# Cross-attention and gated feed-forward on one core: attention by 8 heads at a time, and a reordered query stage

## The chip, the cores and the metric

The kernel runs on one core of a Trainium2 chip. Its engines are TensorE (PE, with PEld for its weight loads), VectorE (DVE), ScalarE (ACT), GpSimd (POOL) and SyncE (SP, which issues most DMAs). Each engine takes its instructions in order and waits on semaphores for the others. The metric is the device time of one execution in microseconds (us), the median of several runs.

## What is computed

x is 16 x 128 x 1024 (16 blocks of 128 tokens), the context has the same shape; all is float32. Attention has 32 query heads of 32 channels in 8 groups, so that four query heads share one key and value head. Cut to what matters:

```python
def attn(q, k, v, w_q, w_k, w_v, w_out, mask):
    query, key, value = q @ w_q.T, k @ w_k.T, v @ w_v.T      # 32 heads; 8 groups; 8 groups
    scores = einsum('bghnd,bgsd->bghns', query, key) / 32**0.5
    scores = where(mask, scores, finfo.min)
    out = einsum('bghns,bgsd->bghnd', softmax(scores), value)
    return out @ w_out.T

x = x + attn(layernorm(x), ctx, ctx, w_q, w_k, w_v, w_out, mask)
x1, x2 = split(layernorm(x) @ w12.T + b12)
x = x + (silu(x1) * x2) @ w3.T + b3
```

## The kernel before

All large matrix products are done by fast schemes that trade a matrix product for sums of operands: seven products of half-sized parts in place of eight ("seven", numbers 1 to 7), in the query product and the first feed-forward product on two levels. A left sum (of weights or numbers) is named S or A_S, QS, QI; a right sum (of the streamed matrix) is named Y, Y_T, ctx_T or wo_T. These sums are made by DVE (through `nc.vector`) and POOL (through `nc.gpsimd`).

**The stages in time.** The first context products (keys and values of the first 8 blocks, `seven_round` with T = 0) end at about 58 us. The query stage follows, to about 246 us: 14 steps (`Q_STEPS`: outer number i in the order 1, 2, 3, 6, 5, 7, 4, for g = 0 and 1), each with seven inner products in the order 1, 5, 6, 7, 2, 3, 4, about 12 us of PE. Then attention, to about 612 us: for each of 16 token blocks t and each half gh of the heads, scores, softmax, turning and values; between these pieces PE works off a stream of other products, the second half of the context (`seven_round` with T = 1) and the output projection (`O_round`). The rest is the output projection's end and the feed-forward part.

**The query stage.** What goes with a step is written as a plan: `q_at(n, j, fn)` calls fn after product j of step n, and `q_follow` does it; n = -1 is the last context round. Within this stage the order on PE, DVE, ACT, POOL and SP is that of the program text. `q_outer_left(g)` makes the outer left sums 5, 6, 3, 7 of the query weights on POOL and stores them, with the parts for 2 and 4, to DRAM by six to eight DMAs on SP's queue (L517, L520); `q_load_left` (L193 through `load`) brings back the sum of a step two steps ahead; `q_inner_left` makes four inner left sums on POOL (L303, QI). `load_xq` loads the parts of x in turned form (xq). `q_outer_right` makes outer right sums on DVE (L488; its result overwrites an xq part or is a Y), `q_inner_right` the inner ones on DVE (L496, Y_T). In `seven`, L285 copies a bank, L288 and L290 make u1 and u3 from banks, and `done` in `q_step` adds to the kept sums (L579, L581, L586, L588). `centre(i)` takes the weights' mean off the query weights: sums on ACT, one matmul (L453), eight DVE instructions (L456). `feed_ctx` gives, in steps 11 to 13, one piece after another of the second context's loads and right sums (L243, two on DVE and two on POOL by pairs), with the loads and left sums of `wkv` put in between.

**Attention.** `scores(t, gh)` takes 16 heads: four banks, one for each of the key heads gl = 0 to 3; the loop runs over j (four query heads) outside and gl inside, so consecutive matmuls (L710) lie on rows 0, 32, 64, 96 onward of the array:

```python
for j in range(HPG):
    for gl in range(GL):
        rows = ds(gl * DH, DH)
        nc.tensor.matmul(
            ps[gl][:, j, :], QT[T, gh * HPG + j][rows, c, toks], KT[T, c][rows, gh, toks],
```

Then, for two banks at a time, DVE scales and masks (L719) and takes the maximum (L722), ACT makes the exponentials and their sums (L728), DVE the reciprocal (L734) and POOL scales the numbers (L737). `flip` turns the numbers of one gl (four transposes on PE, L743) and copies them out of the bank, on ACT (L746) or DVE (L748), to a temporary. `values` multiplies with V (L758, eight listed matmuls on four column groups), and ACT copies the result (L762). In the main loop an iteration takes the scores of one (t, gh), the values of two before, and the four flips of the one before; `stream.run(cost)` in between lets PE work off about so many us of the stream. A listed pair of matmuls of one kind is one float32 matmul of the program.

Buffers: 44 units of 1024 numbers for each partition, 14 temporaries of 512, 8 PSUM banks, each handed out in turn and waited for when all are taken.

Of the kernel before, what the change touches and what calls it, by code (L numbers as in the profile page):

```python
# [11 lines left out]
F32 = mybir.dt.float32  # L12
# [116 lines left out]
def xattn_ffn_kernel(  # L129
# [312 lines left out]
    def centre(i):  # L442


        ws, rows = raw_q[i], rows_in.pop(i)
        total = small.tile([P, 4], F32, tag="wm_sum", name=f"wm_sum_{i}", bufs=2)
        spread = temp([HC, P], f"wm_{i}")
        for r in range(4):
            nc.scalar.activation(rows[r], rows[r], AF.Identity, accum_out=total[:, r : r + 1])
            nc.scalar.activation(spread[:, r], ident, AF.Identity, scale=total[:, r : r + 1])  # L450
        yield 0.0
        ps = bank(f"wm_{i}").rearrange("p (r f) -> p r f", r=HC)
        nc.tensor.matmul(ps, mean_of, spread, start=True, stop=True)  # L453
        for q in range(4):
            for c in range(2):
                nc.vector.scalar_tensor_tensor(ws[q][:, :, c], ws[q][:, :, c], QSCALE, ps, ALU.mult, ALU.subtract)  # L456
        yield 0.87


# [17 lines left out]
    def q_outer_right(i, h, c):  # L477
        B11, B12, B21, B22 = (xq.get((2 * K + h, 2 * C + c)) for K in range(2) for C in range(2))
        y = Y.setdefault(i, {})
        if i in (1, 2, 3):  # L480
            y[h, c] = {1: B11, 2: B21, 3: B22}[i]
            return
        out, x, z = {
            5: (B11, B12, B11), 6: (None, B22, Y.get(5, {}).get((h, c))), 7: (B12, B22, B12),
            4: (B21, B21, Y.get(6, {}).get((h, c))),
        }[i]
        y[h, c] = out if out is not None else unit([2, 512], f"Y6_{h}_{c}")
        nc.vector.tensor_sub(y[h, c], x, z)  # L488

# [7 lines left out]

    q_left, q_inner, q_dram = {}, {}, {}

# [4 lines left out]
    def q_outer_left(g):  # L504
# [3 lines left out]
        for k, a, op, b in (  # L508
            (5, A21, "+", A22), (6, S[5], "-", A11), (3, A12, "-", S[6]), (7, A11, "-", A21),
        ):  # L510
            for h in range(2):
                x, z = (t[:, h] if t in (S[5], S[6]) else t[h] for t in (a, b))
                put(nc.gpsimd, S[k][:, h], x, op, z)
        for k in (2, 3, 6, 5, 7, 4):
            t = q_dram[g, k] = tc.dram_tile([P, 2, 2, 2, P], F32, name=f"QS{k}_dram_{g}")
            if k in S:
                nc.sync.dma_start(t, S[k])  # L517
            else:
                for h in range(2):
                    nc.sync.dma_start(t[:, h], {2: A12, 4: A22}[k][h])  # L520

# [4 lines left out]
    def q_inner_left(g, i, k):  # L526
        if i == 1:
            q_left[g, i] = q_part(g, 0, 0)
        A11, A12, A21, A22 = (q_left[g, i][h][:, r] for r in range(2) for h in range(2))
# [73 lines left out]
    def q_plans():  # L603
        for n, (g, i) in enumerate(Q_STEPS):
            if i != 1:
                q_at(n - 2, 3, q_load_left, g, i)
# [4 lines left out]
            if i == 1:  # L611
                q_at(0 if g else -1, 7, q_outer_left, g)
                q_at(n + 1, 2, q_store, g, i, "U")
# [36 lines left out]
        for m in (0, 1, 4, 5):  # L650
            q_at(12, 1 + m, q_home, 0, m)
        for j in range(1, 8):
            q_at(11, j, feed_ctx)
            q_at(12, j, feed_ctx)
            q_at(13, j, feed_ctx)

    def feed_ctx():
        if "ctx_1" not in feeds:
            feeds["ctx_1"] = Feed(ctx_work[1], 0)
        feeds["ctx_1"].give(1)  # L660

# [14 lines left out]
    def seven_round(T, k, R):  # L676
# [10 lines left out]
        def hook(j):  # L687
            tick()
            if (T, k, j) == (1, 0, 4):
                sums_left7(1, 1)  # L690
            if T == 1 and j in (1, 3):
                load_xs(NT + 2 * k + j // 2)
            if T == 1 and j in (4, 6):
                q_stats(NT + 2 * k + j // 2 - 2)
            transition(T, k, j)

        order = (1, 5, 6, 2, 7, 3, 4) if T else (1, 2, 5, 6, 7, 3, 4)
        yield from seven(left7.pop((T, k)), R, f"Q7_{T}_{k}", done, hook, order)

    OT, spilled = {}, {}  # L700

    def scores(t, gh):

        T, (c, i) = t // NT, divmod(t % NT, 4)
        toks, rstd = ts(i, S), mr[T][:, 1, t % NT : t % NT + 1]
        ps = [bank(f"s_{t}_{gh}_{gl}").rearrange("p (h k) -> p h k", h=HPG) for gl in range(GL)]
        for j in range(HPG):
            for gl in range(GL):
                rows = ds(gl * DH, DH)
                nc.tensor.matmul(  # L710
                    ps[gl][:, j, :], QT[T, gh * HPG + j][rows, c, toks], KT[T, c][rows, gh, toks],
                    start=True, stop=True,
                )
        numbers = []
        for two in range(2):
            nmax = small.tile([P, 2, HPG], F32, tag="nmax", name=f"nmax_{t}_{gh}_{two}")
            for e in range(2):
                s = ps[2 * two + e]
                nc.vector.scalar_tensor_tensor(  # L719
                    s, s, rstd, drop.unsqueeze(1).to_broadcast([P, HPG, S]), ALU.mult, ALU.add,  # L720
                )
                nc.vector.tensor_reduce(nmax[:, e], s, AX.X, ALU.max, negate=True)  # L722
            total = small.tile([P, 2, HPG], F32, tag="sum", name=f"sum_{t}_{gh}_{two}")
            for e in range(2):
                gl = 2 * two + e
                p = temp([HPG, S], f"p_{t}_{gh}_{gl}")
                for j in range(HPG):
                    nc.scalar.activation(  # L728
                        p[:, j, :], ps[gl][:, j, :], AF.Exp, bias=nmax[:, e, j : j + 1],
                        accum_out=total[:, e, j : j + 1],  # L730
                    )
                numbers.append(p)
            inv = small.tile([P, 2, HPG], F32, tag="inv", name=f"inv_{t}_{gh}_{two}")
            nc.vector.reciprocal(inv, total)  # L734
            for e in range(2):
                p = numbers[2 * two + e]
                nc.gpsimd.tensor_mul(p, p, inv[:, e].unsqueeze(2).to_broadcast([P, HPG, S]))  # L737
        return numbers

    def flip(bt, gh, gl, p):  # L740
        pt = bank(f"pt_{bt}_{gh}_{gl}").rearrange("p (h k) -> p h k", h=HPG)
        for j in range(HPG):
            nc.tensor.transpose(pt[:, j, :], p[:, j, :], ident)  # L743
        pT = temp([HPG, S], f"pT_{bt}_{gh}_{gl}")
        if gl % 2:
            nc.scalar.copy(pT, pt)  # L746
        else:
            nc.vector.tensor_copy(pT, pt)  # L748
        return pT

    def values(t, gh, pTs):

        T, (c, i) = t // NT, divmod(t % NT, 4)
        if gh == 0:
# [38 lines left out]
    def O_round(r):  # L793
# [4 lines left out]
        def hook(j):  # L798
# [3 lines left out]
            if j == (6 if r < EARLY else 5) and r + 1 < B // 2:  # L802
                left_O(r + 1)
            if r < 2 and j in (1, 3):
                load_xs(NT + 4 + 2 * r + j // 2)
            if r < 2 and j in (4, 6):
                q_stats(NT + 4 + 2 * r + j // 2 - 2)
            if r == 4 and j == 1:
# [100 lines left out]
    wo_R, wo_work = seven_right(loader(wo, "wo"), "wo", nc.gpsimd)  # L909
    ctx_work[1].insert(1, (4, lambda: load_left7(1)))  # L910
    ctx_work[1].insert(4, (2, lambda: sums_left7(1, 0)))
    wo_work.insert(5, (4, lambda: load_pair(0)))
# [47 lines left out]
    with tc.manual_schedule(engines={ENGINES.PE, ENGINES.DVE, ENGINES.Activation, ENGINES.Pool, ENGINES.SP}):  # L960
        stream.add(*(q_step(n) for n in range(len(Q_STEPS))))
        stream.finish()
    feeds["ctx_1"].finish()

    pending = ready = None
    for T in range(2):
        if T == 0:
            stream.add(*(seven_round(1, k, ctx_R[1]) for k in range(2)))
            stream.add(*(O_round(r) for r in range(2)))
            share = 98.0 / NT / GH  # L970
        else:
            stream.add(*(O_round(r) for r in range(2, EARLY)))
            share = (24.1 * (EARLY - 2) - 12.0) / NT / GH
        for i in range(NT * GH):
            t, gh = T * NT + i // GH, i % GH
            p = scores(t, gh)
            if (t, gh) in ((NT - 1, 0), (NT - 1, 1)):
                for m in range(HPG):
                    q_home(1, gh * HPG + m)
            stream.run(share * 0.25)  # L980
            if ready is not None:
                values(*ready)
            stream.run(share * 0.15)
            pTs = []
            for gl in range(GL):
                if pending is not None:
                    pTs.append(flip(*pending[:2], gl, pending[2][gl]))
                stream.run(share * 0.15)
            if pending is not None:
                ready = (*pending[:2], pTs)  # L990
            pending = (t, gh, p)
        if T == 0:
            stream.finish()
    stream.run(3.0)
    values(*ready)
    stream.run(5.0)
    pTs = []
    for gl in range(GL):
        pTs.append(flip(*pending[:2], gl, pending[2][gl]))
        stream.run(2.5)  # L1000
    stream.finish()
    values(*pending[:2], pTs)


# [372 lines left out]
```

## Time and profile before

| | us |
|---|---|
| median of 3 runs | 1195.07 |
| lowest, highest | 1194.06, 1196.31 |
| the profiled execution | 1195.93 |
| its span in the profile | 1194.1 |

| row | count | mean ns of one |
|---|---|---|
| L719 DVE, scale and mask | 128 | 750 |
| L722 DVE, maximum | 128 | 679 |
| L728 ACT, exponential | 512 | 405 |
| L737 POOL, scale the numbers | 128 | 1065 |
| L743 PE, transposes | 512 | 278 |
| L710 PE, scores (two rows) | 768 + 256 | 291, 270 |
| L758 PE, values | 256 | 606 |

The span runs from the first instruction to the last; 1.8 us of the profiled execution lie around it. [...] what one costs PE is read from the distance of starts, or from the chain of waits, whose pieces do not overlap. "xN" counts instructions. "[2.71 <-DVE Y_T L496]" in a timeline means that the engine was idle for 2.71 us before, until DVE's instruction of that line ended. PEclk is the granted clock of TensorE; a wait named with POOL or DVE is the last semaphore before the start that the profile could find.

### The profile page before, as it was taken

Reading aid. Unit: us, or ns where it says so; the run is one execution under the profiler, and the core shown is the slowest. Engines: PE = TensorE matmul, PEld = TensorE weight load, DVE = VectorE, ACT = ScalarE, POOL = GpSimd, SP = SyncE. Lnnn points to the kernel's source line nnn. Section 1 sums busy time; section 2 is a strip of 40 time slices with the busy share of each in tenths; the row PEclk is TensorE's granted clock in tenths of the full one; section 3 lists DMA queues with packets and bytes.
Section 4 is the critical chain, followed back from the end, with each engine's and each line's share of the span. In section 5 each row is a group of like instructions: output and inputs, shape, how many; then the busy total and the mean of one; then the engine's idle time right before and its main releaser. Section 6 shows DMA issues by size and latency. Waiting matters only on the chain.

```text
span 1194.1 us, 13638 instructions
## 1 busy us (share of the span) xinstructions
PE 1158.4 (97%) x4232; PEld 538.1 (45%) x4232; DVE 872.1 (73%) x1224; ACT 377.3 (32%) x1395; POOL 619.9 (52%) x575
## 2 busy tenths in 40 slices
PE   9997999899999999999999999999999999999998
PEld 4443444345444444445454454444444444444443
DVE  4565899987968878777738445666777786979872
ACT  1210000047577577766644221210011012211210
POOL 5563343845576546556536437572432442457465
PEclk9998999999999999999999999999999999999999
DMA  9689976902335422230467599968833879362511
GB/s 365 256 328 327 300 202 267 297 17 107 141 136 201 160 93 103 107 124 19 142 248 283 190 355 329 257 222 271 204 106 125 246 191 283 107 223 109 178 71 70
DMA packets 71672, 231.61 MB, mean 194 GB/s; under 512 B 7984, under 2 KB 7984, under 8 KB 71600
## 3 DMA queue, kind: packets, MB, share of 16 engines
q1 hardware_dynamic: 64688, 206.10, 46.7%
q0 software_dynamic: 6048, 22.02, 9.8%
q10 hardware_dynamic: 864, 2.62, 0.6%
q8 instruction: 34, 0.56, 0.2%
q14 instruction: 38, 0.31, 0.1%
HBM read 142.63 MB, written 78.64 MB: 185 GB/s over the span
## 4 chain that ended last, share of the span: by engine, by line
PE 76%; DVE 7%; ACT 4%; issue 2%; DMA 1%; POOL 0%; SPq 0%; ACTq 0%; DVEq 0%; POOLq 0%
PE F_b L199 28%; PE G_b L199 15%; PE O_b L199 14%; PE Q_b L199 10%; PE pt L743 4%; ACT p L728 3%; PE s L710 3%; PE o L758 2%; DVE s L719 1%; DMA xs<-in_x_dram 1%; DVE xq L488 1%; PE xt L862 1%; DVE nmax L722 1%; DVE Y_T L496 1%; DVE QUr L579 1%
## 5 line engine op out<-in xcount | busy, mean ns | idle before, releaser
L728 ACT ACTIVATE p<-s,nmax 128x128 f32<-128x128 f32 x512 | 181.7, 405 | 106.2 <-DVE nmax L722 87.8
L737 POOL TENSOR_TENSOR p<-p,inv 128x512 f32<-128x512 f32 x128 | 133.7, 1065 | 141.4 <-DVE inv L734 136.6
L199 PE MATMUL F_b<-X_T,L 128*128 128x512 f32 x304 | 135.7, 592 | 0.0
L728 ACT ACTIVATION_READ_ACCUMULATOR p<-s,nmax 128x1 f32 x512 | 125.1, 244 | 0.0
L199 PE MATMUL G_b<-w_R,A_L 128*128 128x512 f32 x256 | 114.7, 593 | 0.0
L719 DVE SCALAR_TENSOR_TENSOR s<-s,mr,drop 128x512 f32<-128x512 f32 x128 | 90.3, 750 | 25.7 <-PE s L710 25.7
L743 PEld LDWEIGHTS pt<-ident,p 128*128 128x128 f32 x512 | 62.8, 144 | 86.4 <-issue 73.8
L743 PE MATMUL pt<-ident,p 128*128 128x128 f32 x512 | 78.6, 278 | 12.9 <-issue 5.2
L199 PEld LDWEIGHTS F_b<-X_T,L 128*128 128x128 f32 x304 | 57.4, 190 | 70.8 <-issue 69.6
L722 DVE TENSOR_REDUCE nmax<-s 128x4 f32<-128x512 f32 x128 | 81.7, 679 | 0.0
L303 POOL TENSOR_TENSOR x<-x,G_n 128x512 f32<-128x512 f32 x36 | 50.9, 1437 | 50.5 <-DVE G_n L366 31.8
L199 PEld LDWEIGHTS G_b<-w_R,A_L 128*128 128x128 f32 x256 | 48.6, 190 | 61.6 <-issue 59.3
L285 ACT COPY F_p<-F_b 128x512 f32<-128x512 f32 x28 | 16.4, 586 | 187.7 <-PE F_b L199 187.7
L384 ACT COPY G_c<-G_b 128x512 f32<-128x512 f32 x52 | 30.5, 586 | 140.7 <-PE G_b L199 136.0
L1140 DVE TENSOR_TENSOR M<-F_u,F_b 128x512 f32<-128x512 f32 x57 | 38.9, 684 | 45.8 <-PE F_b L199 43.4
L199 PE MATMUL Q_b<-Y_T,QI 128*128 128x512 f32 x152 | 68.3, 594 | 2.2 <-DVE Y_T L496 2.2
L303 POOL TENSOR_TENSOR x<-x,G_c 128x512 f32<-128x512 f32 x36 | 52.6, 1478 | 31.9 <-DMA x<-x_dram 13.2
L199 PE MATMUL O_b<-wo_T,O_S 128*128 128x512 f32 x128 | 67.8, 630 | 0.9 <-ACT p L728 0.9
L199 PE MATMUL O_b<-wo,O_S 128*128 128x512 f32 x128 | 64.3, 611 | 0.3 <-ACT p L728 0.3
L199 PE MATMUL F_b<-xnT,L 128*128 128x512 f32 x128 | 60.8, 592 | 0.0
L199 PE MATMUL O_b<-wo,OTr 128*128 128x512 f32 x112 | 57.2, 609 | 0.0
L288 DVE TENSOR_TENSOR F_u<-F_b,F_p 128x512 f32<-128x512 f32 x28 | 19.3, 691 | 45.3 <-PE F_b L199 41.7
(237 smaller groups left out, 2244.3 us busy)
## 6 DMA issues: line engine op xcount, KB each, us to landing
w<-in_w_dram SPq DMA_DIRECT2D x36, 512.0 KB, 6.4
xq<-in_xT_dram SPq DMA_DIRECT2D x16, 512.0 KB, 9.2
xs<-in_x_dram SPq DMA_DIRECT2D x16, 512.0 KB, 6.7
xp<-in_x_dram SPq DMA_DIRECT2D x16, 512.0 KB, 6.0
x_dram<-xp SPq DMA_DIRECT2D x16, 512.0 KB, 3.0
xn_dram<-xn SPq DMA_DIRECT2D x16, 512.0 KB, 2.9
xnr<-xn_dram SPq DMA_DIRECT2D x16, 512.0 KB, 5.6
h<-hT_dram SPq DMA_DIRECT2D x16, 512.0 KB, 6.0
```

Source lines behind the costliest of these rows:

```text
L199: nc.tensor.matmul(ps, lhsT, rhs, start=start and i == 0, stop=stop and i == len(pairs) - 1, skip_group_check=True,)
L288: nc.vector.tensor_add(u1, banks[6], p1)
L303: (eng.tensor_add if op == "+" else eng.tensor_sub)(out, a, b)
L384: nc.scalar.copy(t, ps)
L710: nc.tensor.matmul(ps[gl][:, j, :], QT[T, gh * HPG + j][rows, c, toks], KT[T, c][rows, gh, toks], start=True, stop=True,)
L719: nc.vector.scalar_tensor_tensor(s, s, rstd, drop.unsqueeze(1).to_broadcast([P, HPG, S]), ALU.mult, ALU.add,)
L722: nc.vector.tensor_reduce(nmax[:, e], s, AX.X, ALU.max, negate=True)
L728: nc.scalar.activation(p[:, j, :], ps[gl][:, j, :], AF.Exp, bias=nmax[:, e, j : j + 1], accum_out=total[:, e, j : j + 1],)
L737: nc.gpsimd.tensor_mul(p, p, inv[:, e].unsqueeze(2).to_broadcast([P, HPG, S]))
L743: nc.tensor.transpose(pt[:, j, :], p[:, j, :], ident)
L758: nc.tensor.matmul(o[ds(gl * DH, DH), :, :], V[T, c][:, i, ts(gh * GL + gl, DH)], pTs[gl], start=True, stop=True,)
L1140: nc.vector.tensor_add(dst, s, ps)
```

## The change

Query stage:

- `centre(1)` takes the mean off the first two quarters at once and off the other two at (0, 5).
- The outer right sums of `q_outer_right` go to POOL, except for i = 5.
- `q_outer_left` stores nothing any more. A new function `q_keep_left` stores the part for 4 before the sums are made, sums 3 and 6 after step g's product 7, sums 5 and 7 a step later. The part for 2 is neither stored nor loaded: step i = 2 reads the query weights in place.
- `feed_ctx` goes. The loads of the second context come at steps 10, 11 and 13, those of `wkv` at 12, and the four right sums with the left sums behind the last step.

Attention:

- `scores(t, gh, two)` takes two of the four gl, two banks; the rest of it is as before.
- The main loop has twice as many iterations, each with the scores of 8 heads and two flips, of the part two before; values follow when both parts of a (t, gh) are turned. The turned numbers lie in a unit instead of temporaries. The share of the stream for each iteration is half, and in the second half of the blocks the sum of shares is 6.0 smaller.
- The loads and statistics of x for T = 1 all come in `seven_round`; the order of its products is 1, 2, 5, 6, 7, 3, 4 for both T.

```diff
@@ centre
-        for q in range(4):
-            for c in range(2):
-                nc.vector.scalar_tensor_tensor(ws[q][:, :, c], ws[q][:, :, c], QSCALE, ps, ALU.mult, ALU.subtract)
         yield 0.87
...
+        if i == 0:
+            take(0, 1, 2, 3)
+        else:
+            take(0, 1)
+            q_at(0, 5, take, 2, 3)
@@ q_outer_right
-        nc.vector.tensor_sub(y[h, c], x, z)
+        (nc.vector if i == 5 else nc.gpsimd).tensor_sub(y[h, c], x, z)
@@ q_outer_left
-        for k in (2, 3, 6, 5, 7, 4):
+        q_sums[g] = S
+
+    def q_keep_left(g, *ks):
+        for k in ks:
             t = q_dram[g, k] = tc.dram_tile([P, 2, 2, 2, P], F32, name=f"QS{k}_dram_{g}")
-            if k in S:
-                nc.sync.dma_start(t, S[k])
+            if k == 4:
+                for h in range(2):
+                    nc.sync.dma_start(t[:, h], q_part(g, 1, 1)[h])
             else:
-                for h in range(2):
-                    nc.sync.dma_start(t[:, h], {2: A12, 4: A22}[k][h])
+                nc.sync.dma_start(t, q_sums[g][k])
@@ q_inner_left
-        if i == 1:
-            q_left[g, i] = q_part(g, 0, 0)
+        if i < 3:
+            q_left[g, i] = q_part(g, 0, i - 1)
@@ q_plans
-            if i != 1:
+            if i > 2:
                 q_at(n - 2, 3, q_load_left, g, i)
...
             if i == 1:
-                q_at(0 if g else -1, 7, q_outer_left, g)
+                q_at(g - 1, 7, q_keep_left, g, 4)
+                q_at(g - 1, 7, q_outer_left, g)
+                q_at(g, 7, q_keep_left, g, 3, 6)
+                q_at(g + 1, 2, q_keep_left, g, 5, 7)
...
-        for j in range(1, 8):
-            q_at(11, j, feed_ctx)
-            q_at(12, j, feed_ctx)
-            q_at(13, j, feed_ctx)
+        for n, e in ((10, 0), (11, 5), (13, 1), (13, 3)):
+            q_at(n, 1, lambda e=e: ctx_work[1][e][1]())
+        q_at(12, 1, load_left7, 1)
@@ scores
+        gls = (2 * two, 2 * two + 1)
+        ps = {gl: bank(f"s_{t}_{gh}_{gl}").rearrange("p (h k) -> p h k", h=HPG) for gl in gls}
         for j in range(HPG):
-            for gl in range(GL):
+            for gl in gls:
...
@@ main
-    feeds["ctx_1"].finish()
+    for e in (2, 4, 6, 7):
+        ctx_work[1][e][1]()
+        if e == 2:
+            sums_left7(1, 0)
...
+    def flip_next(cost):
+        t, gh, two, ps = pending.popleft()
+        for e in range(2):
+            flip(t, gh, two, e, ps[e])
+            stream.run(cost)
+        if two:
+            ready.append((t, gh))
...
-            share = 98.0 / NT / GH
+            share = 98.0 / NT / GH / 2
...
-            share = (24.1 * (EARLY - 2) - 12.0) / NT / GH
+            share = (24.1 * (EARLY - 2) - 18.0) / NT / GH / 2
-        for i in range(NT * GH):
...
+        for i in range(NT * GH * 2):
+            t, gh, two = T * NT + i // GH // 2, i // 2 % GH, i % 2
+            pending.append((t, gh, two, scores(t, gh, two)))
...
+            stream.run(share * 0.35)
+            if ready:
+                values(*ready.popleft())
             stream.run(share * 0.25)
...
+            if len(pending) > 2:
+                flip_next(share * 0.2)
```

## The prediction

> **What bounds the kernel now.** I read the engines' shares first, then the busy time by stage, then the waits of PE, then short timelines.
>
> ```profile
> PE 1158.4 (97%) x4232; PEld 538.1 (45%) x4232; DVE 872.1 (73%) x1224; ACT 377.3 (32%) x1395; POOL 619.9 (52%) x575
> ...
> PEclk9998999999999999999999999999999999999999
> ```
> ```profile
> 58.00:246.00 188.00, 175.40 (x398) 75.85 (x396) 156.00 (x188) 17.13 (x34) 95.89 (x89) 0.97 0.83 280
> 246.00:612.00 366.00, 349.93 (x2261) 174.32 (x2261) 286.68 (x521) 237.83 (x1142) 210.13 (x204) 0.98 0.32 120
> ```
>
> The columns are window, its length, then busy us of PE, PEld, DVE, ACT, POOL, the granted clock, the DMA share and GB/s. PE is the bound: what adds PE work lengthens the kernel, and only PE's waits can be won back. The query stage (58 to 246 us) and attention (246 to 612) hold nearly all of them; after 612 PE is never idle for long.
>
> PE's pitch is steady: the chain has 508 F_b matmuls in 218.28 us, 0.430 each; eight transposes take 0.87, 0.109 each. Attention holds 453 L199 matmuls (194.7 us), 512 + 16 transposes (57.6), 32 score blocks and 32 value blocks. The timeline prices the blocks:
>
> ```profile
> 264.44 1.02 PE L199 MATMUL Q_b<-ctx,wkv 128*128 128x512 f32 x2
> 265.39 0.73 PE L710 MATMUL s<-K,Q 32*128 32x128 f32 x16
> 265.94 0.62 PE L710 MATMUL s<-K,QUr 32*128 32x128 f32 x16
> 266.50 1.13 PE L199 MATMUL Q_b<-ctx,wkv 128*128 128x512 f32 x2
> 267.55 1.07 PE L758 MATMUL o<-pT,V 128*32 128x512 f32 x8
> 268.55 1.13 PE L199 MATMUL Q_b<-ctx,A_S 128*128 128x512 f32 x2
> ```
>
> First column start, second duration. A block of 32 score matmuls runs from 265.39 to 266.50: 1.10 us, not 32 x 0.109 = 3.5, because matmuls on 32 rows run side by side on four row groups. The two L199 before it hold PE 0.95 instead of 0.86, so entering a block costs 0.1 more: 1.2 each. A value block takes 1.0 plus 0.2 at its entry. Sum: 194.7 + 57.6 + 38.4 + 38.4 = 329; the other **37 us** of attention are waits and half clock (16 show as idle, the rest as stretched matmuls).
>
> **Heads, 8 at a time (L703 to L738).** Each call now has gl 0,1 or gl 2,3: two row groups. Matmuls of one row group follow each other, four heads x two passes = 8 slots, whether two or four groups are filled; 1.10 us is these 8 slots (8 x 0.11) and the drain. So half the heads cost a whole block. Between two halves stand other matmuls on all rows (stream.run), so halves cannot share slots. 32 more blocks x 1.2 = **+38.4 us on PE**, on the path. DVE, ACT and POOL instructions stay as they are (128 L719 and L722, 512 exponentials, 128 L737), as do the transposes.
>
> **Turned two parts later.** The gain: two score banks instead of four, and looser lags. Of the 37 us of waits, 3 stand at the start (priced below), so 34 at most can go. Bounds: none, and all. DVE has 286.68 us of work for 366; with PE at some 400 that is 72%, and one half's chain is short: two L719 and two L722 2.7 (247.62 to 250.2 in the timeline), eight exponentials with their reads 2.8, two L737 2.0, with queueing, which I put at half as much again, some 11 us against 2.6 halves x 5.9 = 15 until the transposes. So most waits of the transposes (L743, the longest) should go; those of L710 and L199 for a bank that ACT or DVE still reads should go in part, for 8 banks still serve two score blocks under work, one transpose, one value block and three or four products. I take **-20**. The buffers for turned numbers move from temps to units; loads have slack (DMA share 0.32): nothing, or some us where units run short.
>
> **Query stage, early.** The longest PE wait of the run:
>
> ```profile
> 89.55 0.44 SPq L193 DMA_DIRECT2D xq<-in_xT_dram  x1
> ...
> 94.43 1.23 DVE L488 TENSOR_TENSOR xq<-xq,xq 128x1024 f32<-128x1024 f32 x1 [7.11 <-DMA xq<-in_xT_dram]
> ...
> 99.84 2.90 PE L199 MATMUL Q_b<-xq,QI 128*128 128x512 f32 x3 [6.31 <-POOL QI L303]
> ```
>
> The row names POOL, but this product adds to a bank that DVE's L290 reads first, and L290 ended at 99.74, behind the L488 that had waited 7.11 us for xq. That load was issued at 89.55 only: SP's queue stood behind the QS stores, which waited for POOL's sums until 80.96, and the QU stores. In the changed order of SP the QS5 and QS7 stores come a step later, S2 is neither stored nor loaded (step i=2 reads raw_q, three transfers less for each g), and the xq loads stand behind the QU stores of step 0, whose sums L586 ended at 73.4 in this trace. Each sum is still stored a step before its load. Gain: 6.3, 0.6 of entry, and 2.9 of half clock after it (144 matmuls in 64.82 us, 61.9 at 0.43). The centring of g=1 in two halves lets L586 through between them: the 1.3 wait and its 0.6 go. Together **-11.7**; below that only if xq still lands late.
>
> **Query stage, late.**
>
> ```profile
> 224.13 2.88 DVE L243 TENSOR_TENSOR ctx_T<-ctx,ctx 128x1024 f32<-128x1024 f32 x2
> ...
> 230.55 2.67 PE L199 MATMUL Q_b<-Y_T,QL 128*128 128x512 f32 x4 [2.71 <-DVE Y_T L496]
> ...
> 235.68 4.50 DVE L243 TENSOR_TENSOR ctx_T<-ctx,ctx_T 128x1024 f32<-128x1024 f32 x2
> ...
> 239.17 5.98 POOL L243 TENSOR_TENSOR ctx_T<-ctx,ctx_T 128x1024 f32<-128x1024 f32 x2 [1.22 <-DVE ctx_T L243]
> ```
>
> DVE is the limit here (29.02 busy of 180 to 210), and PE waits 4.9 us for Y_T in three places. The change takes 12 outer sums (L488, 1.2 to 2.0 us each, some 20) and the four ctx sums off this stretch. POOL gets 12 x 2.8 = 34 us, ahead of the QI sums in its queue; the Y sums mostly wait for nothing, and a step of 12 us holds four QI sums (3 to 5) and two Y sums (5.6), so QI comes in time. The Trainium skill speaks against it: "SBUF — State Buffer", section "SBUF: two separate sides", has DVE with two SBUF inputs and POOL exclude each other for a whole instruction. The rows show both: beside short POOL sums DVE's 1.2 becomes 1.74, but the two L243 at 235.68 take 4.50 while POOL's ran. By 1.74, 12 sums cost DVE 12 x 0.5 = 6 of the 20; by the lock up to 12 x 2.1 = 25, no relief at all. Half of DVE's instructions here read PSUM, so I take some 11. A second rule: "TensorE: Matmul & The Clock Gate", "What's actually happening", gives half clock after an idle window of about 3.4 us. The row says less suffices: after the 2.71 wait four matmuls took 2.67, and the four at 233.01 took 2.94, where four take 1.88. By the rule the wait is worth 2.7, by the rows 4.0; I use the rows. All of it is 4.9 + 0.5 entry + 1.3 = 6.7, none is zero: I take **-5**.
>
> **Start of attention.**
>
> ```profile
> 252.93 2.04 POOL L737 TENSOR_TENSOR p<-p,inv 128x512 f32<-128x512 f32 x2 [7.78 <-DVE inv L734]
> ...
> 260.42 0.63 PE L743 MATMUL pt<-ident,p 128*128 128x128 f32 x4 [1.70 <-ACT p L728]
> ```
>
> The ctx sums now come at the end of the query stage, and on POOL they stand ahead of the first L737. Let E be the end of the last Q_b matmul (246.2). POOL then has R7's first half 2.8 (it waits for DVE's R5, about E-1), eight A_S sums (0.72 to 1.2 each, 6 to 10), 2.8, and R4's two 5.6: free at E+17 to E+21, where before the first L737 began at E+6.7. PE reaches the first transpose after three score blocks (3 x 1.2) and, by its order in the changed kernel, seven pairs of L199 (7 x 0.86 = 6.0), at about E+9.5. It waits 7.5 to 11.5, and half clock follows, 1.7 to 2.9. Before, this place cost 2.7. Net **+8** (bounds 3, if POOL's sums start earlier, and 12).
>
> **Costed at nothing:** the xs loads and L208 earlier (DVE has 20% free), load order of ctx and wkv (DMA), and 6 us of PE work moved behind the last half by the smaller share: PE does it anyway, unless it leaves the last transposes bare (2 us).
>
> **Sum.** 38.4 - 20 - 11.7 - 5 + 8 = +9.7 on the profiled execution's 1195.9 (span 1194.1 and 1.8 around it): 1205.6. The median of the runs is 0.9 lower, so 1205.
>
> **Rivals.**
> - *Waits stay* (1224): DVE, ACT and POOL do the same work in the same order, so PE meets them as often; only 5 of 34 go, the start costs 11, late query gains 2: 38.4 - 5 - 11.7 - 2 + 11 = +30. For it: PE's idle in attention is spread over some 35 small places. Against: PE now takes longer per half than every other engine.
> - *Banks freed sooner* (1189), on the other side: with two banks per part the score and transpose waits of attention vanish almost whole. Place: 246 to 612. Price: 32 of 34 gained; the start costs 3, the late query stage gains all 6.7. 38.4 - 32 - 11.7 - 6.7 + 3 = -9, and 0.2% of dispersion about it. It decides from where the waits regained pass 30 of 34 with my other terms. For it: the lag of 15 us against 11. Against: at 97% busy little but the fill is ever regained whole.
> - *Row groups cost nothing* (1168): if one group's slots could overlap with the next part's, 38.4 falls to about 0. Against: the L199 matmuls between on 128 rows.
>
> **Chances.** Forecast 0.60 (its own range 1196 to 1215), waits stay 0.22, banks freed 0.15, row groups 0.03. A measurement here tells about 0.2% (2.4 us) from no change; the runs of before lie 2.3 apart. Faster: 0.15 + 0.03 = 0.18; within 0.2%: 0.07, the forecast's lower edge; slower: 0.53 + 0.22 = 0.75. The range takes in the banks case and the waits case: 1188 to 1226.
>
> **What would show it.** Right: score blocks of 16 matmuls at 1.1 us, 64 of them, PE's work in attention near 367 us; no wait of PE near 93 and xq's load issued before 82; PE waiting 6 us or more for L737 at the first transposes. Wrong: blocks of 16 at 0.6 us (the 38.4 falls), attention with under 5 us of waits, or POOL's QI sums named as PE's new wait in the query stage.

## The result and the profile after

The changed kernel takes **1214.66 us** (median of 4 runs, 1214.08 to 1215.78), the one before 1194.57 in the same comparison (4 runs, 1191.93 to 1196.31): a ratio of 1.0171, 95% interval 1.0151 to 1.0192, so some 20 us slower. The span grew from 1194.1 to 1214.0 us. The head of the page shows where not to look for it:

```profile
PE 1188.5 (98%) x4232; PEld 569.4 (47%) x4232; DVE 865.5 (71%) x1214; ACT 379.7 (31%) x1393; POOL 641.9 (53%) x587
...
PEclk9999999979999999999999999999999999999999
```

PE's share even rose, with the same 4232 matmuls: PE is not idle more, it does the same matmuls in more time. The busy time by stage (window, length, then PE, PEld, DVE, ACT, POOL, granted clock, DMA share, GB/s) splits it, with the borders where the stages now lie:

```profile
58.00:236.00 178.00, 171.58 (x399) 75.61 (x398) 141.23 (x173) 16.57 (x32) 103.36 (x90) 0.98 0.86 287
236.00:620.00 384.00, 371.66 (x2220) 199.66 (x2220) 290.12 (x514) 238.83 (x1136) 220.22 (x209) 0.98 0.27 100
```

The query stage ends at 236 instead of 246 us. DVE has 15 us less of it, POOL 7 more. Attention ends at 631 instead of 610 us. The waits of PE are few now, and two of them make up most:

```profile
PE pt L753 <- POOL p L744: 8.3, 1, 8.3
PE Q_b L199 <- DVE Y_T L506: 6.4, 1, 6.4
PE s L720 <- DVE pT L756: 2.8, 1, 2.8
```

Columns: who waits for whom, us in total, times, longest. The wait for POOL's QI at 93 us and the waits of the transposes for ACT (4.2 us before) are gone.

**One score block.** The timeline (start, duration) at an undisturbed place:

```profile
265.12 1.02 PE L199 MATMUL Q_b<-ctx_T,A_S 128*128 128x512 f32 x2
266.07 0.71 PE L720 MATMUL s<-K,Q 32*128 32x128 f32 x8
266.62 0.61 PE L720 MATMUL s<-K,QUr 32*128 32x128 f32 x8
267.16 1.13 PE L199 MATMUL Q_b<-ctx_T,A_S 128*128 128x512 f32 x2
```

From 266.07 to 267.16: 16 matmuls hold PE for 1.09 us. Before, 32 held it for 1.10. Half the work costs the whole block.

**The difference in parts.** For each matmul I took the distance to the next start and subtracted the steady pitch of its kind (0.43 for a product, 0.109 for a transpose, 1.10 and 1.0 for a score and a value block). A duration alone would not do: a product is listed with 0.59 us, and the next one starts 0.43 after it. What is left, called "over pitch" below, is wait, half clock, or the small cost of entering a block. Summed by place, in us:

| place | before | after | difference | forecast |
|---|---|---|---|---|
| up to 58 us | 5.0 | 5.4 | +0.4 | 0 |
| query stage, 58 to 110 us | 11.2 | 0.0 | -11.2 | -11.7 |
| query stage, the rest | 7.9 | 8.7 | +0.8 | -5 |
| 32 more score blocks of 1.104, with 1.5 more for entering | | | +36.8 | +38.4 |
| first 30 us of attention | 3.7 | 13.4 | +9.7 | +8 |
| rest of attention, without that 1.5 | 43.4 | 27.3 | -16.1 | -20 |
| after the last value block, to the start of the last matmul (length) | 578.9 | 578.4 | -0.5 | 0 |
| sum | | | +19.9 | +9.7 |

The parts add up to the difference of the spans.

### The profile page after: what moved, and what is told of

Its sections match the earlier page's. It is cut to its first block, busy times and chain, and to the rows that moved or that the text cites. A ratio compares the mean times of both kernels' runs of the same rounds, so it can differ in the third digit from the quotient of the medians.

```text
span 1214.0 us, 13535 instructions
## 1 busy us (share of the span) xinstructions
PE 1188.5 (98%) x4232; PEld 569.4 (47%) x4232; DVE 865.5 (71%) x1214; ACT 379.7 (31%) x1393; POOL 641.9 (53%) x587
## 4 chain that ended last, share of the span: by engine, by line
PE 90%; DVE 4%; DMA 2%; issue 2%; ACT 1%; POOL 1%; SPq 0%; DVEq 0%; POOLq 0%; ACTq 0%
PE F_b L199 25%; PE Q_b L199 21%; PE O_b L199 16%; PE G_b L199 15%; PE s L720 5%; PE pt L753 4%; PE o L766 3%; PE xt L866 1%; DMA M<-U_dram 1%; ACT p L736 1%; DVE s L727 1%; DVE ctx_T L243 0%; DVE nmax L730 0%; DMA xnr<-xn_dram 0%; POOL ctx_T L243 0%
## 5 line engine op out<-in xcount | busy, mean ns | idle before, releaser
L744 POOL TENSOR_TENSOR p<-p,inv 128x512 f32<-128x512 f32 x128 | 132.3, 1055 | 139.6 <-DVE inv L742 110.6
L736 ACT ACTIVATION_READ_ACCUMULATOR p<-s,nmax 128x1 f32 x512 | 113.5, 222 | 0.0
L727 DVE SCALAR_TENSOR_TENSOR s<-s,mr,drop 128x512 f32<-128x512 f32 x128 | 89.7, 744 | 12.3 <-PE s L720 11.7
L753 PE MATMUL pt<-ident,p 128*128 128x128 f32 x512 | 74.7, 276 | 8.3 <-POOL p L744 8.3
L303 POOL TENSOR_TENSOR x<-x,G_n 128x512 f32<-128x512 f32 x36 | 50.8, 1436 | 48.0 <-DVE G_n L366 28.3
L303 POOL TENSOR_TENSOR x<-x,G_c 128x512 f32<-128x512 f32 x36 | 52.0, 1461 | 34.8 <-ACT G_c L384 31.6
L720 PEld LDWEIGHTS s<-K,Q 32*128 32x128 f32 x768 | 49.0, 187 | 36.5 <-issue 21.6
L720 PE MATMUL s<-K,Q 32*128 32x128 f32 x768 | 61.6, 289 | 2.9 <-DVE pT L756 2.8
L199 PE MATMUL O_b<-wo_T,O_S 128*128 128x512 f32 x128 | 63.9, 606 | 0.0
```

The source lines that it names most:

```text
L199: nc.tensor.matmul(ps, lhsT, rhs, start=start and i == 0, stop=stop and i == len(pairs) - 1, skip_group_check=True,)
L303: (eng.tensor_add if op == "+" else eng.tensor_sub)(out, a, b)
L720: nc.tensor.matmul(ps[gl][:, j, :], QT[T, gh * HPG + j][rows, c, toks], KT[T, c][rows, gh, toks], start=True, stop=True,)
L727: nc.vector.scalar_tensor_tensor(s, s, rstd, drop.unsqueeze(1).to_broadcast([P, HPG, S]), ALU.mult, ALU.add,)
L736: nc.scalar.activation(p[:, j, :], ps[gl][:, j, :], AF.Exp, bias=nmax[:, e, j : j + 1], accum_out=total[:, e, j : j + 1],)
```

## The experiments

Each kernel is made of exact parts of the change, or is the changed kernel with one or a few edits. Intervals are of the ratio to the kernel before; "query stage ends" is the start of the first score matmul in the trace.

### Attention alone, and the query part alone

`att_only` is the kernel before with the attention half of the diff; `q_only` is the kernel before with the query half, attention by 16 heads.

> The attention part of the change alone, on the query stage of before. If a score block costs its 8 slots and its drain however few row groups are filled (my theory), PE gets 32 blocks x 1.15 = 37 us more, and some 15 us of attention's waits go: about 1216 us. If the changed kernel's loss comes from the new waits of its query stage and of the start of attention (rival), this one has none of them and stands near 1200 us or below.

> The query part of the change alone, with the attention of before. Theory: the early waits go (-11.5), the wait for DVE near the end of the stage is replaced by one as long (+1.5), and the start of attention waits for POOL's context sums (+5 to +9): 1190 to 1194 us. Rival (moving the outer sums to POOL and the context sums to the end are gains in themselves, lost only beside attention by 8 heads): 1183 us or less.

`att_only` took 1215.87 us (1.0178, 1.0155 to 1.0201), `q_only` 1192.4 (0.998, 0.9966 to 0.9993). Both times met the theory. The slowdown comes with the attention half. The query half is worth only 2 us, though its trace has the early wait gone. What takes the gain back can be seen there: the wait of 6.4 us for Y_T, and 10.3 us over pitch in the first 30 us of attention (before: 3.7). In that place the theory's mechanism did not come: PE waits only 0.9 us there for POOL's numbers, but 3.5 us for score banks that ACT still reads, because DVE, which had context sums of its own to do, takes up the first scores 7.6 us after they began (before: 1.4).

### Score matmuls of both halves issued together

```diff
+        if two == 0:
+            for gl in range(GL):
+                joined[gl] = bank(f"s_{t}_{gh}_{gl}").rearrange("p (h k) -> p h k", h=HPG)
+        ps = joined
-        for j in range(HPG):
-            for gl in gls:
+        for j in range(HPG if two == 0 else 0):
+            for gl in range(GL):
```

> The changed kernel with the score matmuls of both halves issued together into four banks, in the order of before; softmax, turning and values stay by 8 heads. Theory: 32 score blocks again, all four row groups filled, so PE has 37 us less; part of the waits returns as four banks are held: 1180 to 1195 us. Rival (the loss is in the pace of DVE, ACT and POOL by halves, not in PE's slots): within 5 us of the changed kernel, 1210 or more.

It took 1188.44 us (0.9956, 0.9939 to 0.9973), 26 less than the changed kernel: all else of the change is in it, only the two halves' matmuls stand together. Its timeline:

```profile
268.13 0.73 PE L725 MATMUL s<-K,Q 32*128 32x128 f32 x16
268.68 0.62 PE L725 MATMUL s<-K,QUr 32*128 32x128 f32 x16
269.24 1.12 PE L199 MATMUL Q_b<-ctx,A_S 128*128 128x512 f32 x2
```

32 matmuls from 268.13 to 269.24, 1.11 us, so a block on four row groups costs the same as one on two. Attention is 27.3 us shorter (367.5 against 394.8): 32 blocks fewer are worth 35.3 and its first 30 us 2.9, but the rest of attention has 39.8 us over pitch instead of 28.8. So the smaller waits of the changed kernel belong to the smaller parts.

### Outer right sums back on DVE, all or one step of them

`dve_sums` makes every sum of `q_outer_right` on DVE, `one_back` only those of step i = 4 more:

```diff
-        (nc.vector if i == 5 else nc.gpsimd).tensor_sub(y[h, c], x, z)
+        (nc.vector if i in (5, 4) else nc.gpsimd).tensor_sub(y[h, c], x, z)
```

> The changed kernel with all outer right sums on DVE again. Theory (DVE's sums with two operands in SBUF are shut out while POOL's long sums run): PE's wait of 6.4 us for Y_T and the half clock behind it, 9.5 us together, go, and waits for DVE of 2 to 4 us come back: 1207 to 1209 us. Rival (the DVE instruction of 7.4 us was late for another reason, and DVE is short of time): no gain or a loss, 1214 to 1220 us.

> The changed kernel with the four outer sums of i = 4 on DVE again, those of 6 and 7 still on POOL. Theory (one place: POOL's three long sums in a row shut DVE out at 200 to 207 us): PE's 6.4 us wait and its half clock go, and POOL's other eight sums still spare DVE: 1204 to 1207 us, no slower than with all sums back on DVE. Rival (any long sum on POOL does it, another place takes over): 1210 or more.

`dve_sums`: 1208.35 us (1.0126, 1.0104 to 1.0149), as expected. `one_back`: 1209.08 (1.0142, 1.0118 to 1.0166), 2 us above its range. In both the wait of 6.4 us is gone, and the query stage ends at 228.2 and 230.1 us instead of 236.1 (2.5 of the 7.9 us of `dve_sums` lie before 58 us); DVE's relief was worth less than nothing. Why, the timeline of the changed kernel shows:

```profile
197.83 0.69 DVE L290 TENSOR_TENSOR Q_u<-Q_b,Q_u 128x512 f32<-128x512 f32 x1
...
199.47 7.43 DVE L594 TENSOR_TENSOR QUr<-QUr,Q_u 128x512 f32<-128x512 f32 x1
...
200.34 2.94 POOL L498 TENSOR_TENSOR xq<-xq,Y 128x1024 f32<-128x1024 f32 x1
...
202.64 1.31 POOL L303 TENSOR_TENSOR QI<-QL 128x256 f32<-128x256 f32 x1
...
203.33 2.92 POOL L498 TENSOR_TENSOR xq<-xq,Y 128x1024 f32<-128x1024 f32 x1
...
210.62 1.22 DVE L506 TENSOR_TENSOR Y_T<-xq,xq 128x1024 f32<-128x1024 f32 x1
...
211.98 5.35 PE L199 MATMUL Q_b<-Y_T,QI 128*128 128x512 f32 x8 [6.40 <-DVE Y_T L506]
```

L594 adds two SBUF operands, as do POOL's sums. It takes 7.43 us instead of 0.69 and ends at 206.90, 0.65 after POOL's second L498. What stands behind it on DVE, five more sums into QUr and the first L506, comes late, and PE waits for that Y_T. L290, of the same size and with one operand in PSUM, takes 0.69 as ever. The long L594 is no accident of one execution: it takes 7.42 to 7.44 us in `q_only`, `joined` and `ctx_late` as well, and the longest takes 2.18 in `one_back`. With the sums back on DVE, the group of L594 (count, busy us, mean ns) and the engines' busy time over the whole run are, in `dve_sums`:

```profile
L594 DVE TENSOR_TENSOR QUr<-QUr,Q_u 128x512 f32<-128x512 f32 x18 | 13.5, 750 | 0.6
...
PE 1183.4 (98%) x4232; PEld 566.7 (47%) x4232; DVE 868.2 (72%) x1226; ACT 379.6 (31%) x1393; POOL 619.9 (51%) x575
```

against a mean of 1238 ns, and 865.5 us of DVE, in the changed kernel. So POOL took 20.1 us of outer sums off DVE (L498 on DVE: 26.4 us in `dve_sums`, 6.3 in the changed kernel), and DVE's busy time fell by 2.7: the rest went into longer DVE instructions, 8.8 us of it into L594. That taking the sums of i = 4 off POOL removes the long L594 is shown by `one_back`. How POOL holds it is read from one place: L594 is listed from 0.87 us before the first L498, while POOL issued two DMAs, and which of POOL's instructions held it first is not shown.

That `one_back` missed its range is due to another place: its query stage gained 6 us, as thought, but the part after attention is 3.9 us longer, with a wait of a feed-forward product for a left sum of POOL (F_b for L303, 1.9 us) and a stretch of 3.41 us at half clock behind it, from 795.4 us. The same wait stands in `att_only`, `joined`, `ctx_late` and `all_three`, not in the changed kernel. What decides it stays open.

### The late context sums given out later

Two of the four context sums follow the score parts of the first block:

```diff
-    for e in (2, 4, 6, 7):
+    for e in (2, 4):
...
             pending.append((t, gh, two, scores(t, gh, two)))
+            if i in (2, 3) and T == 0:
+                ctx_work[1][i + 4][1]()
```

> The changed kernel with the context's last four right sums on POOL given out behind the third and fourth score part; in POOL's order the two of number 4 now stand behind the first two L744. Theory (the first transpose waits for POOL's queue): the first L744 comes 5.6 us sooner, PE's 8.3 us wait falls to about 3, and half clock with it: 1206 to 1209 us. Rival (the chain of DVE and ACT is what is late there): 1212 or more.

1211.32 us (1.0154, 1.0127 to 1.0182): a gain of 3, less than expected, between the two ranges, and not clear of noise (the changed kernel's interval is 1.0151 to 1.0192). The trace tells more. PE's waits:

```profile
PE pt L753 <- POOL p L744: 4.1, 1, 4.1
...
PE F_b L199 <- POOL L L303: 1.9, 1, 1.9
```

The first transposes wait for 4.1 instead of 8.3 us, and the first 30 us of attention carry 7.0 over pitch instead of 13.4. The part after attention gives 3.6 of these 6.4 back, with the F_b wait named above among it. The 4.1 that are left are the rival's. `A_S` and R7's second half still stand ahead of the first L744, but POOL is done with them and waits for DVE's reciprocal:

```profile
245.45 2.35 POOL L243 TENSOR_TENSOR ctx<-ctx,ctx 128x1024 f32<-128x1024 f32 x1
248.08 2.04 POOL L744 TENSOR_TENSOR p<-p,inv 128x512 f32<-128x512 f32 x2 [0.29 <-DVE inv L742]
```

DVE has its own context sums ahead of the first scores. In the kernel before its first L719 came 1.4 us after the first score matmul (246.2), in the changed kernel the same instruction (now L727) came 7.6 us after it (236.1). First before, then after:

```profile
247.62 1.41 DVE L719 SCALAR_TENSOR_TENSOR s<-s,mr,drop 128x512 f32<-128x512 f32 x2
```
```profile
242.07 1.74 DVE L243 TENSOR_TENSOR ctx_T<-ctx,ctx_T 128x1024 f32<-128x1024 f32 x1
243.74 1.41 DVE L727 SCALAR_TENSOR_TENSOR s<-s,mr,drop 128x512 f32<-128x512 f32 x2
...
248.76 0.20 DVE L742 RECIPROCAL inv<-sum 128x8 f32<-128x8 f32 x1
```

So in the changed kernel POOL's queue accounts for the last 4.4 us of the 8.3 (248.96 to 253.32), and the chain of DVE and ACT, late by DVE's context sums, for the part before. Giving out more of POOL's sums later would not have brought the first transposes sooner.

### All three edits together

> The changed kernel with the score matmuls of both halves together, the sums of i = 4 on DVE and the context's sums on POOL later. Theory: the gains add, 1188.4 - 8 - 6 = 1174 us, faster than before and after. Rival (with PE relieved, DVE or ACT is the bound of attention and takes the gain back): 1182 or more.

1182.26 us (0.9906, 0.9886 to 0.9926), by its time in the rival's range. Its query stage ends at 229.5, as in `one_back`, but the start of attention keeps 9.3 us over pitch. Its timeline:

```profile
235.05 0.49 PE L725 MATMUL s<-K,Q 32*128 32x128 f32 x4
...
235.40 1.74 DVE L243 TENSOR_TENSOR ctx_T<-ctx,ctx_T 128x1024 f32<-128x1024 f32 x1
237.06 1.40 DVE L732 SCALAR_TENSOR_TENSOR s<-s,mr,drop 128x512 f32<-128x512 f32 x2
...
240.70 0.79 PE L725 MATMUL s<-K,Q 32*128 32x128 f32 x2 [5.16 <-ACT p L741]
```

The second set of four score banks needs a bank that the first still holds, and that set comes free late because DVE does context sums, with the last query sums between them, until 237.06, before its first L732. `joined` has this wait as well (5.15 us). With joined scores the wait for POOL was no longer the last one in this place, so giving out POOL's context sums later could win little there (9.3 us over pitch, in `joined` 10.5): here two edits that each take away a wait of one place did not add up.

### The early half of the query change alone

`early_only` is the kernel before with the later stores, S2 in place and the split centring, and nothing else of the change.

> Before, with only the later stores, the sum for 2 read in place and the centring of g=1 in two halves; outer sums on DVE, context sums and attention as before. Theory: the long wait near 93 us, its half clock and the wait for QM go, nothing else changes: 1183 to 1185 us. Rival (the wait only moves to where DVE is late next, as in the query part alone): 1190 us or more.

**1177.82 us (0.9883, 0.9858 to 0.9908)**: faster than both kernels by more than was expected, and the fastest of this study. What is left over pitch in its query stage is the late part:

```profile
PE Q_b L199 <- DVE Y_T L506: 4.9, 3, 2.7
```

Against before, by the table's method: 58 to 110 us 0.0 (-11.2), the late query stage 7.0 (-0.9), attention 42.9 (-4.2), the first 58 us 3.1 (-1.9). The expectation counted the first two; the 6 us more lie in attention and before 58 us. Most of it can be found in the trace as clock. The 1.9 us before 58 are luck, not the edits' doing: in each trace the first products run either at 0.46 us each or slower, whatever was edited (2.8 to 3.1 us over pitch in five of the twelve traces, 4.6 to 5.4 in the others). First before, then `early_only`:

```profile
4.75 7.49 PE L199 MATMUL Q_b<-ctx,wkv 128*128 128x512 f32 x11 [0.78 <-DMA wkv<-in_wkv_dram]
```
```profile
4.71 3.67 PE L199 MATMUL Q_b<-ctx,wkv 128*128 128x512 f32 x8 [0.74 <-DMA wkv<-in_wkv_dram]
```

In attention the kernel before has four stretches of 3.41 us at half clock (from 317.0, 419.4, 535.5 and 583.3 us), `early_only` two (from 246.9 and 403.9): some 3.4 of the 4.2 us. It is no matter of the one trace: the granted clock was 0.993 to 0.998 in the four runs of `early_only` and 0.990 to 0.993 in the seven of before beside them. Why fewer of attention's waits were followed by half clock is not shown; the last section has what the traces tell of it. Which of the three early edits takes away the early wait was not tried.

### Both attentions on the early half

`early_joined` adds the changed attention, turned two parts later, but with joined score matmuls; `early_att` adds the changed attention as it is.

> The early half of the query change (later stores, S2 in place, split centring) with attention turned two parts later, but with the score matmuls of a whole (t, gh) issued together into four banks; outer right sums and context sums stay as before. Theory (32 score blocks cost what they did; what the joined kernel still paid was the 6.4 us wait for DVE in the query stage and the wait for POOL's context sums at the start of attention): both are gone, so close to the early half alone, 1178, less a few us for the looser lag of the flips: 1170 to 1179, a query stage that ends near 232 and no wait over 4 us for POOL at the first transposes. Rival (with four banks held by the scores the looser lag itself makes attention wait for banks): 1182 or more, with attention longer than the early half's 360.0 by 4 us or more.

> The early half of the query change with the changed attention (scores by 8 heads, 64 blocks), without the outer right sums on POOL and the context sums at the end. Theory (the parts add up): the early half alone, 1177.8, plus what the attention part cost alone, 1215.9 - 1194.8 = 21: 1195 to 1202, so some 15 us less than the changed kernel, which is what outer sums on POOL and context sums at the end cost beside the early half. Rival (the late half of the query change pays for the changed attention, by leaving DVE or POOL free at its start): 1208 or more.

`early_att`: 1204.56 us (1.0076, 1.0052 to 1.0101), 2.6 above the theory's range and 3.4 below the rival's. `early_joined`: 1182.71 (0.9902, 0.9869 to 0.9936), outside the theory's range and in the rival's by its time. Its attention is 2.1 us longer than that of the early half (362.1), half of what the rival asked, and the intervals of the two kernels overlap, so no cost of the lag is shown. What is shown is that the lag, with the other edits of attention but without the halved parts, gains nothing: over pitch, attention has 42.9 us in `early_only`, 44.9 with the lag, and 30.0 with the lag and the halved parts. The waits regained come with two banks at a time. (Whether halved parts without the longer lag would do was not tried.)

In `early_att` the context sums are back in the query stage, and the first transposes find their numbers ready. POOL and PE in its timeline:

```profile
241.33 2.04 POOL L750 TENSOR_TENSOR p<-p,inv 128x512 f32<-128x512 f32 x2 [7.10 <-DVE inv L748]
...
244.10 0.60 PE L759 MATMUL pt<-ident,p 128*128 128x128 f32 x4
```

POOL waits 7.10 us for DVE there, instead of PE for POOL; the first 30 us carry 1.9 over pitch.

The ladder of ratios gives the whole change in four steps: early half 0.9883; with the changed attention 1.0076; with the context sums at the end of the query stage as well (`dve_sums`) 1.0126; with the outer sums on POOL 1.0171. Times 1194 us, that is about -14, +23, +6 and +5. The last two are near the width of the intervals; the traces name a wait for each.

## Why the prediction came out as it did

The direction was right and the time lay in the range, but at the upper edge of what the forecast gave itself (1196 to 1215): the sum is 10 us short, 5.8 of it in the late query stage and 3.9 in attention's waits. Term by term:

- **Score blocks, +38.4: right.** "Half the heads cost a whole block" holds: 1.09 us for 16, 64 of them, +36.8. `joined` shows it as the cause. The rival in which row groups cost nothing is out.
- **Attention's waits, -20: the mechanism in part, the size 4 us too large.** Measured -16.1. The prediction gave two reasons, "two score banks instead of four, and looser lags". `early_joined` leaves the lag no gain; the smaller parts make it. After the first 30 us of attention PE's idle time fell from 13.7 to 4.0 us, and the stretches at half clock from four to one, worth some 5 us. Of the 4.0 us, 2.8 are a score block that waits for DVE's copy of turned numbers, a wait that the prediction had left to its "in part".
- **Query stage, early, -11.7: right.** Measured -11.2. The xq loads are issued at 74.53 and from 75.80 us on (forecast: before 82), and PE runs through:

```profile
75.80 7.07 SPq L193 DMA_DIRECT2D xq<-in_xT_dram  x3
...
84.99 5.31 PE L199 MATMUL Q_b<-Y_T,QI 128*128 128x512 f32 x12
...
90.14 1.88 PE L199 MATMUL Q_b<-xq,wq 128*128 128x512 f32 x4
```

- **Query stage, late, -5: wrong, +0.8, and this is the term that failed most.** The prediction weighed two prices for DVE beside POOL's sums: 1.74 instead of 1.2 for a DVE sum, from a row, and the lock of the Trainium skill ("SBUF — State Buffer", section "SBUF: two separate sides"), no relief at all. It took the middle, "some 11". Measured, it is 17: of 20.1 us moved, DVE kept 2.7 as relief, near the lock's end of the bounds. (DVE's busy time in the stage fell by 15 us, but 12 of them are there in `dve_sums` too, without the move; most of that is the context sums.) And the prediction spread over the stage a cost that falls on single instructions: one L594 was shut out for 6.7 us, and the order behind it set PE's next product. The page has the loser blocked until the winner's instruction ends; here DVE did not get through before the third of three POOL instructions in a row had ended. `dve_sums` has 3.2 us over pitch in this stage, -4.7 against before: moving the context sums alone earns the -5, and the outer sums on POOL took it all back. (Its price for half clock after the 2.7 us wait was too low as well: 2.67 and 2.94 us where four products take 1.88 are 1.8 us more, not 1.3.)
- **Start of attention, +8: the size right, +9.7, the path in part.** POOL was the last to come, as the prediction had it, with the A_S and context sums ahead of the first L744:

```profile
246.41 2.34 POOL L243 TENSOR_TENSOR ctx<-ctx,ctx 128x1024 f32<-128x1024 f32 x1
248.71 4.64 POOL L243 TENSOR_TENSOR ctx_T<-ctx,ctx_T 128x1024 f32<-128x1024 f32 x2
253.32 4.03 POOL L744 TENSOR_TENSOR p<-p,inv 128x512 f32<-128x512 f32 x4
254.41 1.12 PE L753 MATMUL pt<-ident,p 128*128 128x128 f32 x4 [8.32 <-POOL p L744]
```

The first L744 begins 17 us after the last query product (236.1), forecast 17 to 21. What the prediction left out is that DVE's half of the context sums stands ahead of the first scores too: the reciprocal was ready at 248.96 us, so without POOL's queue about half of the wait would have stayed, as `ctx_late` shows.

- **The rival "waits stay"** let only 5 us of attention's waits go; 16.1 went, so it is out, though its time (1224) is as near to the result as the forecast's. **"Banks freed sooner"** named what does free them, and had twice the amount (32). Their sums are a little off: +30.7 on 1195 is 1226, not 1224, and -9 is 1186, not 1189, which is below the stated range.

## What to carry to other kernels

Price a block of matmuls on some rows of the array by what one row group has to do: here 16 matmuls on two row groups held PE for 1.09 us and 32 on four for 1.10, eight on each group in both, so halving the groups halved the work and not the time, and issuing the halves together won it back. (Other numbers of groups or matmuls were not tried.) Price a sum that is moved from a busy engine to a free one by what it does to the busy engine's other instructions: here 20.1 us moved to POOL relieved DVE by 2.7, and the place of one DVE instruction that took 7.43 us instead of 0.69, not the engine's share, set the cost. Where sums are moved to a later place, look at every engine that has them in its queue: here POOL's were priced, and DVE's delayed the same numbers. When a change has a good half and a bad one, run the halves alone: here the early half by itself beats both kernels by 1.2 to 3%.

## What the runs showed of the hardware that was not expected

**Several locks in a row.** L594's 7.43 us reaches over two POOL sums of 2.9 us and a QI sum of 1.31 between them; this DVE instruction was held for longer than any one POOL instruction ran. Two others in the same trace ended 0.5 to 1.1 us after one POOL sum (an L594 of 2.18 us at 151.61, an L506 of 2.50 at 102.96).

**Whether a wait brings half clock depends on where it falls.** The prediction read from before that a wait of 2.7 us costs some 1.3 us of half clock. In `early_only` the same wait, 2.71 us for Y_T, cost none. The half-clock stretches of a trace lie on a raster of 3.41 us (in the kernel before they begin at 98.59, 231.71 and 317.05 us, which are 39 and 25 times 3.413 apart), the free-running window that the Trainium skill describes ("TensorE: Matmul & The Clock Gate", section "What's actually happening"). Two windows of the kernel before, around its wait at 227.8 to 230.6 us (the figure after the window's length is PE's busy us; the third from the end is the granted clock):

```profile
228.30:231.71 3.41, 1.16 (x3) 0.68 (x4) 3.39 (x4) 0.00 (x0) 3.41 (x3) 1.00 1.03 417
231.71:235.12 3.41, 3.41 (x5) 1.35 (x4) 3.11 (x3) 0.00 (x0) 3.41 (x3) 0.50 1.03 423
```

and three of `early_only`, around its wait at 214.8 to 217.5:

```profile
212.79:216.21 3.42, 2.00 (x5) 0.57 (x3) 3.38 (x4) 0.00 (x0) 3.42 (x4) 1.00 1.01 353
216.21:219.62 3.41, 2.12 (x5) 1.06 (x6) 3.38 (x4) 0.00 (x0) 3.41 (x5) 1.00 1.02 419
219.62:223.03 3.41, 3.41 (x9) 1.52 (x8) 3.38 (x4) 0.59 (x1) 3.41 (x2) 1.00 0.95 388
```

In the first case one window was busy for 1.16 us only, and the next ran at half clock; in the second the wait lay across a border, both windows were busy for 2.0 and 2.1 us, and the clock stayed. A whole idle window is not needed. How much is, the traces do not settle: in the changed kernel a window with PE busy for 1.87 us (from 324.60) was followed by one at half clock, in `early_only` one with 1.51 us (from 301.53) was not. After the 8.3 us wait of the changed kernel half clock lasted four windows, 13.65 us, although PE worked on without a break from 254.41:

```profile
246.10:249.50 3.40, 0.00 (x0) 0.00 (x0) 3.40 (x8) 3.40 (x21) 3.40 (x3) 1.00 0.00 0
249.50:263.20 13.70, 8.79 (x30) 5.33 (x31) 7.19 (x14) 7.38 (x38) 9.88 (x8) 0.50 0.00 0
```
